# The weight sums of each group's next to last key tile: on GpSimd beside the others, or on VectorE behind the step's maxima

## The chip, the cores and the metric

The kernel runs on one core of one Trainium2 chip. The metric is the device time of one execution, in microseconds. Three executions of the kernel before took 1801.5, 1802.37 and 1805.26 us, so its median is 1802.37 us. One more execution was profiled, and every view below comes from that one.

The engines are named as in the profile: PE is TensorE's matmul row and PEld its weight loads, DVE is VectorE, ACT is ScalarE, POOL is GpSimd.

## The reference, cut to what matters

Two layers work on x, a tensor of 2 x 1024 rows of 512 numbers in float32. The first layer adds a small scan block and a gated feed-forward block with a Walsh-Hadamard transform. The second adds causal attention with 16 heads of 32 and a gated feed-forward block with two-of-four sparsity. The change lies in the attention:

```
scores = einsum('bqhe,bkhe->bhqk', q, k) * scale
scores = where(causal, scores, -inf)
attn = softmax(scores, axis=-1)
out = einsum('bhqk,bkhe->bqhe', attn, v)
out = out.reshape(b, l, d) @ W_out.T + b_out
```

The softmax is not formed before it is used. The kernel multiplies v with the unnormalized weights exp(score - maximum), adds the weights up beside that, and divides at the end. The additions of the weights are what the change moves.

## The kernel before, in words

The program has three stages: the first layer (to 658 us of the span), the attention with its projections (658 to 1215 us), and the sparse feed-forward block (to the end).

The attention works on units. A unit u is one batch and one group of four heads, so there are eight units, 0 to 7. Within a unit the queries come in two halves j of 512 columns, and the keys in tiles kt of 128 rows. By the causal mask half 0 meets key tiles 0 to 3 and half 1 meets key tiles 0 to 7, which makes twelve steps per unit (`per` is 12) and 96 steps in all. Step (u, 1, 6) is the next to last of a unit. A unit lasts some 62 us and a step some 5.2 us.

The main loop `for n in range(-ahead, len(second))` writes out one step after another, and `in_program_order` then pins that order on PE, DVE, ACT and POOL: each of these engines executes its own instructions in the order in which the loop wrote them. One pass of the loop does this:

- `weights(u, j, kt)` computes the scores of the step in two PSUM pairs of two heads each (PE `s`, L1226 and L1232). ACT writes their exponentials into two tiles `pt` (L1243), for kt = 0 into the two tiles `acc`. From the query column s on, tiles on the diagonal need the causal mask: POOL sets the forbidden half of a 128 x 128 block to zero with `affine_select` (L1252, two of them per step). For half 1 these are kt = 4 to 7. Half 0 is masked in all its steps, so the mask of a unit's first step works on the new `acc`.
- `gather(*behind)` takes the weights of the step before: PE multiplies them with v into the bank `o` (L1272), and for kt > 0 the two tiles are added to the sums, acc += pt (L1279). For key tile 6 only columns 256 to 511 of the two heads are added, 128 x 512 elements per tile. When a half is done, ACT copies `o` to `att` (L1282).
- `do_first(n + ahead)` runs `maxima` for a step 13 steps ahead: PE scores `m` (L1169), DVE adds the mask on diagonal blocks (L1176) and reduces to `tops` (L1177).
- `one_part(n)` runs a piece of other work, mostly a projection: `pq` (L1122, added up by DVE in L1092 or by ACT in L1087), `pv` (L1047, L1148) or `po` (L1047, L1313). A few passes, named in `quiet`, have none. In three units, the weights of a projection are first combined by four POOL instructions (`sq` and `wqk`, L1099 to L1101 and L1134).
- `what_is_fixed(n)` runs small pieces bound to a step. One is `larger` (L1187), a DVE maximum of 16 columns. It is followed by the `shift_part` pieces on ACT (L1197) and POOL (L1199), and by the transposes `px` (L1207) and their copy `neg` (L1211).

The score pairs of `s` and `m` take turns in three PSUM buffers, so a pair waits until ACT or DVE has read the pair three turns earlier. Parts use one bank, so each waits until the part before has been read. The tiles `pt` have five buffers.

The engine of L1279 is chosen by one line:

```
            if kt:
                eng = nc.vector if idle_vector(u, j, kt) else nc.gpsimd
```

`idle_vector` is true from the point on where no maxima are left, which covers the sums of unit 7. In units 0 to 6 all the sums that the change can touch are on POOL. There, one step of half 1 gives POOL two masks and two sums in this order: the masks of a step, then the sums of the step before.

Of the kernel before, what the change touches and what calls it, by code (L numbers as in the profile page):

```python
# [35 lines left out]
def two_layers(ctx: ExitStack, tc: tile.TileContext, t: dict, out: bass.AP):  # L36
    nc = tc.nc
# [37 lines left out]
    def ps_bank(name, which):  # L75

        return ps.tile([P, 512], F32, tag=f"bank{which}", name=name)
# [278 lines left out]
    with tc.tile_pool(name="a", bufs=1) as a:  # L356
# [431 lines left out]
        for n in range(NU - 1):  # L788
            u = 2 * n + 2
# [162 lines left out]
    with tc.tile_pool(name="b", bufs=1, reuse_waits="tile") as b:  # L952
# [207 lines left out]
        def maxima(u, qt, c):  # L1160

            q, k = qk[u, 0], qk[u, 1]
            if qt == 0:
                tops[u] = sm.tile([P, 2, QT, 4], F32, tag="tops", name=f"tops_{u}", bufs=2)
            e = min((qt + 1) * P - c * 512, 512)
            pair = [ps_wide(f"m_{u}_{qt}_{c}_{p}") for p in range(2)]
            for h in range(4):
                rows = slice(h * HD, (h + 1) * HD)
                nc.tensor.matmul(  # L1169
                    pair[h // 2][:, h % 2, :e], q[rows, qt * P : (qt + 1) * P],  # L1170
                    k[rows, c * 512 : c * 512 + e], start=True, stop=True,
                )
            for p in range(2):
                if c == qt // 4:
                    d = pair[p][:, :, e - P : e]
                    nc.vector.tensor_add(d, d, mask.unsqueeze(1).to_broadcast([P, 2, P]))  # L1176
                nc.vector.tensor_reduce(  # L1177
                    out=tops[u][:, c, qt, 2 * p : 2 * p + 2], in_=pair[p][:, :, :e],
                    axis=mybir.AxisListType.X, op=ALU.max,
                )  # L1180
# [32 lines left out]
        def idle_vector(u, j, kt):  # L1213

            return per * u + 4 * j + kt + ahead >= len(second)
# [40 lines left out]
                got.append(pt)  # L1256
            return u, j, kt, s, got

        held, sums_of = {}, {}

        def gather(u, j, kt, s, pts):

            bb, hg = units[u]
            if kt == 0:
                held[u, j] = ps_bank(f"o_{u}_{j}", 0)
                sums_of[u, j] = pts
            po = held[u, j]
            last = kt == 4 * j + 3
            v = vals[bb, kt // NJ, kt % NJ][:, hg * P : (hg + 1) * P]
            for h in range(4):  # L1270
                rows = slice(h * HD, (h + 1) * HD)
                nc.tensor.matmul(  # L1272
                    po[rows, s:], v[:, rows], pts[h // 2][:, h % 2, s:],
                    start=(kt == 0), stop=last, tile_position=(0, h * HD),
                )
            if kt:
                eng = nc.vector if idle_vector(u, j, kt) else nc.gpsimd
                for acc, pt in zip(sums_of[u, j], pts):
                    eng.tensor_add(acc[:, :, s:], acc[:, :, s:], pt[:, :, s:])  # L1279
            if last:  # L1280
                att[u, j] = b.tile([P, 512], F32, tag="att", name=f"att_{u}_{j}", bufs=12)
                nc.scalar.copy(att[u, j], po)  # L1282
# [136 lines left out]
        def do_first(n):  # L1419
            u, qt, c = first[n]  # L1420
            maxima(u, qt, c)
# [3 lines left out]
        def one_part(n):  # L1425

            if not open_parts:
                ready = [x for x in rest if x[0] <= n]
                if not ready:
                    return False  # L1430
                x = min(ready, key=lambda x: x[1])
                rest.remove(x)
                open_parts.extend(x[2])
            f, *args = open_parts.pop(0)
            f(*args)
            return True

        def what_is_fixed(n):
            for f, *args in fixed.pop(n, ()):
                f(*args)  # L1440
                if f == total:
                    for q in range(4):
                        put(n + 1, divide, *args, q)

        def late(n):

            return any(
                sum(len(x[2]) for x in rest if x[0] <= n and x[1] <= last) + len(open_parts)
                > last - n
                for last in {x[1] for x in rest}  # L1450
            )
# [9 lines left out]
        for n in range(-ahead, len(second)):  # L1461
            if n == 0:
                alone = None
            now = weights(*second[n]) if n >= 0 else None
            for f, *args in middle.pop(n, ()):
                f(*args)
            if behind is not None:
                gather(*behind)
            behind = now
            for f, *args in after.pop(n, ()):  # L1470
                f(*args)
            if n < 0:
                one_part(n)
            if n + ahead < len(first):
                do_first(n + ahead)
            if (n >= 0 or n % 2) and n not in quiet:
                one_part(n)
            while late(n) and one_part(n):
                pass
            what_is_fixed(n)  # L1480
        in_program_order(start)
        gather(*behind)
        alone = 0
        n = len(second)
# [13 lines left out]
    with tc.tile_pool(name="c", bufs=1, reuse_waits="tile") as c_:  # L1498
# [131 lines left out]
        for n in range(groups - 1):  # L1630

            end = n == groups - 2
            u = 2 * n + 2
# [165 lines left out]
```

## Time and profile before

| | before |
|---|---|
| median of three executions | 1802.37 us (1801.5 to 1805.26) |
| the profiled execution | 1803.46 us, span 1801.7 us |
| PE busy | 1776.1 us (99%) |
| DVE busy | 1141.5 us (63%) |
| ACT busy | 480.2 us (27%) |
| POOL busy | 847.8 us (47%) |
| POOL sums (L1279) | 138, 233.7 us |
| DVE sums (L1279) | 22 |
| mean granted TensorE clock | 0.998 |

The span runs from the first to the last instruction in the trace; the profiled execution's own time is 1.76 us longer, which is what lies around the span. A busy share is of the span. A row of the timeline gives start, duration, engine, line, operation, output <- inputs, shape and count, and in brackets the idle time of the engine before it with what ended it. Line numbers are those of the kernel before. A row may join several instructions of one kind.

### The profile page before, as it was taken

The numbers are of one execution on the slowest core, as the hardware profiler recorded it, in microseconds if no ns is written. First come the engines' busy times: TensorE is split into PE (matmuls) and PEld (weight loads), VectorE is DVE, ScalarE is ACT, GpSimd is POOL, SyncE is SP. The second block draws the span as 40 slices with busy tenths as digits, with TensorE's granted clock in tenths as the row PEclk, the third lists the DMA queues.
The fourth block names the chain that finished last, engine by engine and source line by source line (L and its number), as shares of the span: only waits on it lengthen the run. The fifth ranks groups of instructions, "written<-read, shape, count | busy, mean of one in ns | idle before, by whom it ended". The sixth has DMA issues, their size and how long they took to land.

```text
span 1801.7 us, 19007 instructions
## 1 busy us (share of the span) xinstructions
PE 1776.1 (99%) x7354; PEld 910.9 (51%) x7354; DVE 1141.5 (63%) x1502; ACT 480.2 (27%) x687; POOL 847.8 (47%) x741
## 2 busy tenths in 40 slices
PE   9999999999999999999999999999999999999999
PEld 5456566555555564333333333334555555555555
DVE  4875444555544457566666666762867778778676
ACT  3322222122221113433433433422212211212220
POOL 5145553355642244577868866613243344342510
PEclk9999999999999999999999999999999999999999
DMA  6120110111101010000000000011110102211101
GB/s 234 47 82 24 49 45 25 35 35 35 35 24 35 12 41 13 1 12 13 1 24 25 13 12 1 25 47 35 35 59 28 54 24 70 84 34 47 47 1 47
DMA packets 29609, 68.12 MB, mean 38 GB/s; under 512 B 3408, under 2 KB 11856, under 8 KB 27984
## 3 DMA queue, kind: packets, MB, share of 16 engines
q1 hardware_dynamic: 28800, 66.61, 11.1%
q8 instruction: 59, 0.97, 0.2%
q10 hardware_dynamic: 720, 0.30, 0.1%
q14 instruction: 30, 0.25, 0.0%
HBM read 62.70 MB, written 4.19 MB: 37 GB/s over the span
## 4 chain that ended last, share of the span: by engine, by line
PE 90%; POOL 4%; DVE 3%; ACT 1%; issue 1%; POOLq 0%; ACTq 0%; DVEq 0%
PE p_a L183 22%; PE p_c L183 21%; PE d L309 19%; PE m L1169 4%; PE s L1226 3%; PE pv L1047 3%; PE po L1047 3%; PE o L1272 3%; POOL acc L1279 3%; PE pq_a L1122 2%; PE dr L1620 2%; PE pq_c L1122 1%; DVE tops L1177 1%; PE pp L607 1%; PE pw L443 1%
## 5 line engine op out<-in xcount | busy, mean ns | idle before, releaser
L327 POOL TENSOR_TENSOR x<-x,de 128x512 f32<-128x512 f32 x87 | 126.6, 1469 | 297.8 <-DVE x L322 162.5
L1279 POOL TENSOR_TENSOR acc<-acc,pt 128x1024 f32<-128x1024 f32 (+3 forms) x138 | 233.7, 1717 | 0.0
L1177 DVE TENSOR_REDUCE tops<-m 128x2 f32<-128x1024 f32 (+2 forms) x192 | 180.9, 956 | 52.3 <-PE m L1169 47.7
L322 DVE TENSOR_TENSOR x<-x,d 128x512 f32<-128x512 f32 x145 | 99.2, 685 | 143.2 <-PE d L309 142.9
L1243 ACT ACTIVATE pt<-s 128x1024 f32<-128x1024 f32 (+3 forms) x160 | 115.4, 766 | 191.1 <-PE s L1232 174.3
L309 PE MATMUL d<-td,h 128*128 128x256 f32 x592 | 139.2, 379 | 0.0
L309 PEld LDWEIGHTS d<-td,h 128*128 128x128 f32 x592 | 112.5, 190 | 42.6 <-issue 28.7
L183 PE MATMUL p_a<-xt,s_a 128*128 128x512 f32 x256 | 116.6, 598 | 0.0
L183 PE MATMUL p_a<-xt,w 128*128 128x512 f32 x256 | 115.4, 593 | 0.7 <-ACT xt L136 0.7
L183 PE MATMUL p_c<-xt,gu 128*128 128x512 f32 x256 | 115.7, 592 | 0.0
L183 PE MATMUL p_a<-t_a,s_a 128*128 128x512 f32 x256 | 115.3, 594 | 0.0
L183 PE MATMUL p_c<-xt,s_c 128*128 128x512 f32 x256 | 115.1, 592 | 0.0
L1169 PE MATMUL m<-qk,qk 32*128 32x512 f32 (+3 forms) x768 | 104.8, 542 | 4.1 <-ACT acc L1243 3.0
L1176 DVE TENSOR_TENSOR m<-m,mask 128x256 f32<-128x256 f32 x128 | 54.8, 428 | 84.3 <-PE m L1169 76.1
L1226 PE MATMUL s<-qk,qk 32*128 32x512 f32 (+3 forms) x768 | 98.2, 532 | 3.5 <-DVE tops L1177 2.3
L176 POOL TENSOR_TENSOR s_c<-gu,s_c 128x512 f32<-128x512 f32 x16 | 20.4, 1274 | 132.4 <-PE p_c L183 132.4
L1169 PEld LDWEIGHTS m<-qk,qk 32*128 32x128 f32 x768 | 40.4, 184 | 73.6 <-issue 25.0
L183 PEld LDWEIGHTS p_a<-xt,s_a 128*128 128x128 f32 x256 | 47.2, 190 | 57.8 <-issue 57.4
L183 PEld LDWEIGHTS p_c<-xt,s_c 128*128 128x128 f32 x256 | 48.6, 190 | 51.5 <-issue 50.2
L183 PEld LDWEIGHTS p_c<-xt,gu 128*128 128x128 f32 x256 | 48.6, 190 | 51.0 <-issue 49.5
L183 PEld LDWEIGHTS p_a<-xt,w 128*128 128x128 f32 x256 | 48.4, 190 | 50.1 <-issue 47.6
L1226 PEld LDWEIGHTS s<-qk,qk 32*128 32x128 f32 x768 | 34.0, 183 | 78.5 <-issue 67.5
(286 smaller groups left out, 3236.3 us busy)
## 6 DMA issues: line engine op xcount, KB each, us to landing
w<-in_W SPq DMA_DIRECT2D x32, 512.0 KB, 3.5
gu<-in_gu SPq DMA_DIRECT2D x32, 512.0 KB, 3.5
wd<-in_down SPq DMA_DIRECT2D x8, 1024.0 KB, 4.8
x<-in_x SPq DMA_DIRECT2D x16, 256.0 KB, 4.2
w2h<-in_W2q SPq DMA_DIRECT2D x4, 1024.0 KB, 12.0
xr<-in_x SPq DMA_DIRECT2D x16, 256.0 KB, 2.6
wqk<-in_WqkvT SPq DMA_DIRECT2D x16, 256.0 KB, 3.1
out_x<-x SPq DMA_DIRECT2D x15, 256.0 KB, 2.0
```

Source lines behind the costliest of these rows:

```text
L183: nc.tensor.matmul(pair[:, m, :], a[:, m, k, :], x[:, k, :], start=start and k == 0, stop=stop and k == 1, skip_group_check=True,)
L309: nc.tensor.matmul(out_[:, j, :], lhs[:, q, j * P : (j + 1) * P], rhs[:, q], start=m in (0, 1, 3, 4) and j == q == 0, stop=j == q == 1, sk ...
L322: nc.vector.tensor_add(r, r, out_)
L327: nc.gpsimd.tensor_add(r, r, u2[half])
L1047: nc.tensor.matmul(got[0], lhs(k), rhs(k), start=(k == 0), stop=(k == KC - 1))
L1122: nc.tensor.matmul(got[chain], lhs[:, k, :], rhs[k] if type(rhs) is list else rhs[:, k, :], start=start and k == 0, stop=stop and k == 1, ...
L1169: nc.tensor.matmul(pair[h // 2][:, h % 2, :e], q[rows, qt * P : (qt + 1) * P], k[rows, c * 512 : c * 512 + e], start=True, stop=True,)
L1176: nc.vector.tensor_add(d, d, mask.unsqueeze(1).to_broadcast([P, 2, P]))
L1177: nc.vector.tensor_reduce(out=tops[u][:, c, qt, 2 * p : 2 * p + 2], in_=pair[p][:, :, :e], axis=mybir.AxisListType.X, op=ALU.max,)
L1226: nc.tensor.matmul(pair[h // 2][:, h % 2, s:], k[rows, kt * P : (kt + 1) * P], q[rows, cols], start=True, stop=False,)
L1243: nc.scalar.activation(pt[:, :, s:], pair[p][:, :, s:], AF.Exp, scale=1.0 / math.sqrt(HD))
L1279: eng.tensor_add(acc[:, :, s:], acc[:, :, s:], pt[:, :, s:])
```

## The change

The sums of key tile 6 in half 1 of units 0 to 6 are no longer written out by `gather` on POOL. They are kept in a list, and the main loop writes them out on DVE after the maxima of the same pass, ahead of that pass's part. All other sums stay where they were, and so do the masks. In the written order, `larger` comes behind the sums in units 0 to 5, since it is written out at the end of the pass; in unit 6 it is written out one step earlier and stays ahead of them.

```diff
-        held, sums_of = {}, {}
+        held, sums_of, add_later = {}, {}, []
+
+        def add_weights(eng, u, j, s, pts):
+            for acc, pt in zip(sums_of[u, j], pts):
+                eng.tensor_add(acc[:, :, s:], acc[:, :, s:], pt[:, :, s:])
...
-            if kt:
-                eng = nc.vector if idle_vector(u, j, kt) else nc.gpsimd
-                for acc, pt in zip(sums_of[u, j], pts):
-                    eng.tensor_add(acc[:, :, s:], acc[:, :, s:], pt[:, :, s:])
+            if (j, kt) == (1, 6) and not idle_vector(u, j, kt):
+
+                add_later.append((nc.vector, u, j, s, pts))
+            elif kt:
+                add_weights(nc.vector if idle_vector(u, j, kt) else nc.gpsimd, u, j, s, pts)
...
             if n + ahead < len(first):
                 do_first(n + ahead)
+            while add_later:
+                add_weights(*add_later.pop())
             if (n >= 0 or n % 2) and n not in quiet:
                 one_part(n)
```

## The prediction, made blind

> **What bounds the kernel now.** I read the page's busy times first, then busy time by stage, then the chain that ended last around a unit boundary, and last the timelines of PE, POOL and DVE at the boundaries.
>
> ```profile
> PE 1776.1 (99%) x7354; PEld 910.9 (51%) x7354; DVE 1141.5 (63%) x1502; ACT 480.2 (27%) x687; POOL 847.8 (47%) x741
> ```
> ```profile
> 658.00:1215.00 557.00, 538.86 (x3392) 193.59 (x3391) 370.10 (x530) 204.83 (x323) 361.90 (x358) 0.99 0.05 16
> ```
>
> PE sets the time. In the attention (second fence: length, then PE, PEld, DVE, ACT, POOL) it is idle for 557.00 - 538.86 = 18.1 us, so a change to POOL and DVE can bring only part of that, and whatever makes PE wait costs in full. The chain shows where POOL reaches PE, the boundary of units 0 and 1:
>
> ```profile
> 785.41 2.46 POOL acc L1279 x2
> 790.73 0.37 POOL acc L1252
> 791.14 1.41 PE o L1272 x8
> ```
>
> Half 1 gives POOL more work than a step holds: it falls behind, and the first mask of the next unit comes late. The timelines there (PE, POOL, DVE):
>
> ```profile
> 791.14 1.41 PE L1272 MATMUL o<-acc,v 128*32 128x512 f32 x8 [0.74 <-POOL acc L1252]
> ```
> ```profile
> 784.65 0.77 POOL L1252 TENSOR_SCALAR_AFFINE_SELECT pt<-pt 128x256 f32<-128x256 f32 x2
> 785.38 2.50 POOL L1279 TENSOR_TENSOR acc<-acc,pt 128x512 f32<-128x512 f32 x2
> 787.83 0.73 POOL L1099 TENSOR_TENSOR sq<-wqk 128x256 f32<-128x256 f32 x1
> 790.68 0.76 POOL L1252 TENSOR_SCALAR_AFFINE_SELECT acc<-acc 128x256 f32<-128x256 f32 x2
> ```
> ```profile
> 784.09 0.65 DVE L1187 TENSOR_TENSOR tops<-tops 128x16 f32<-128x16 f32 x1
> 786.69 0.43 DVE L1176 TENSOR_TENSOR m<-m,mask 128x256 f32<-128x256 f32 x1 [1.96 <-PE m L1169]
> ```
>
> PE wants the masked acc at 790.40 and gets its first tile at 791.09. It waits 0.74 us, and the two tiles come 0.36 us apart, so the group takes 1.41 us instead of 1.06 as at 852.56. The same stands at 914.96 and 1039.01 (0.76 idle, 1.41 long): the three boundaries where the weight sums (L1099 to L1134) lie before that mask. At 1/2, 3/4 and 5/6 they do not, and POOL is in time: at 850.89, where PE asks at 852.56.
>
> **Off POOL.** The sums are the 128x512 form: half of its 28 instructions on POOL (1276 ns). Fourteen go, 17.9 us busy, 2.46 us per boundary. Only three boundaries wait for them, each for 0.75 + 0.35 = 1.1 us: 3.3 us on the path. Everything else there hides behind PE.
>
> **Onto DVE.** The same form costs on DVE:
>
> ```profile
> L1279 DVE TENSOR_TENSOR acc<-acc,pt 128x512 f32<-128x512 f32 x4 | 2.6, 685 | 0.0
> ```
>
> Fourteen times 0.685 is 9.6 us. They lie where DVE has finished its maxima (784.16) and idles until 786.69, so by length they fit. But they need POOL twice. The first needs POOL's sum of key tile 5 for its own tile (done 782.9), the second the other one (784.70). And both operands lie in SBUF, which the trace shows to be slow beside POOL: `larger`, 16 columns, took 0.165 us at 725.5 with POOL idle, and here:
>
> ```profile
> 907.82 1.44 DVE L1187 TENSOR_TENSOR tops<-tops 128x16 f32<-128x16 f32 x1
> 908.47 0.76 POOL L1252 TENSOR_SCALAR_AFFINE_SELECT pt<-pt 128x256 f32<-128x256 f32 x2
> ```
>
> It ended at 909.26, when POOL's second mask ended (909.23). At 784.09, 1031.87 and 1093.51 it ended with POOL's running sum instead, ahead of the masks; issued during the first mask (847.25, 971.07) it waited for the second too. So DVE gets in at the end of a POOL sum, mostly, and not between two masks.
>
> The Trainium skill, "SBUF — State Buffer", section "Who interferes with whom", says that a DVE instruction with two SBUF inputs and a GpSimd instruction that reads SBUF exclude each other, the later one blocked until the first ends. It speaks against this change, and these rows agree. By the rule taken whole, the masks wait for a whole sum (0.69 us); the total below would then be 1.3 us higher, 1799.9 us.
>
> Step by step at boundary 0/1: the first DVE sum starts with POOL's release at 784.70 and holds the pair for about 0.5 us. That is my estimate: in unit 7 a 256-column DVE operation stretched POOL's pair of sums from 2.50 to 2.68 us, and 685 ns is the upper end; bounds 0.2 and 0.7. The masks of key tile 7 end at 785.9 instead of 785.41. The second DVE sum follows to 786.5, `larger` behind POOL's next instruction to about 787.3. The next maxima start 0.6 us late. PE asks for their first buffer at 789.8, and they free it at 788.5 instead of 787.85: covered, with 1.2 us left. The part's bank at 1/2 and 3/4 (DVE L1148 now behind the sums) is free at 849.4 where PE asks at 849.62: covered by 0.2 us only.
>
> The late masks reach PE: key tile 7's `o` starts at 785.59, its second half at 785.72. Masks 0.5 later hold the second half by 0.24 us, of which 0.18 is hidden, since the next `m` waits until 786.76 for ACT anyway. That leaves 0.06 us, seven times: 0.4 us. Its bounds are nothing (masks first) and 7 x 0.6 = 4.2 us (both sums ahead of the second mask).
>
> What is late next: POOL's queue to the acc mask is now two sums' holds (1.0 to 1.25) and 787.83 to 791.44 (3.6), from 785.4, so it ends by 790.25, the first tile by 789.9. PE asks at 790.40 and 790.7. The stall goes whole, with half a microsecond to spare.
>
> **Unit 7.** Here POOL's sums fight DVE's masks:
>
> ```profile
> 1155.27 2.68 POOL L1279 TENSOR_TENSOR acc<-acc,pt 128x512 f32<-128x512 f32 x2
> ```
> ```profile
> 1155.82 2.41 DVE L1248 TENSOR_TENSOR acc<-acc,allowed 128x256 f32<-128x256 f32 x2 [1.65 <-ACT acc L1243]
> ```
> ```profile
> 1157.34 2.00 PE L1272 MATMUL o<-acc,v 128*32 128x512 f32 x8 [0.42 <-ACT att L1282]
> ```
>
> The pair of masks takes 0.75 us at 1158.86 with POOL idle, 2.41 here. After the change DVE's sums run from 1154.4 to 1156.2 (behind POOL's key tile 5), the masks from 1156.8 to 1157.5, and `o` takes 1.06: it ends at 1158.4 instead of 1159.34. I take 0.9 us; bounds 0 (the later waits for ACT at 1171.71 and DVE at 1179.92 eat it) and 0.9.
>
> **The sum.** 1803.46 - 3.3 - 0.9 + 0.4 = 1799.7 us for the profiled execution. The median stands 1.1 us lower: 1802.4 - 3.8 = 1798.6 us, 0.21% faster. About 0.2% (3.6 us) is what a measurement of this kernel can tell from no change, so the forecast lies just beyond that line.
>
> **Rivals.**
>
> *Slower: POOL keeps the pair until its queue is dry.* At the three boundaries with weight sums POOL runs without a pause from 784.7 to 793.9. If DVE waited that long, the sums would end at 795.2, the first maximum at 796.3 where PE asks at 789.8: 6.5 us, three times, 19.5 - 3.8 gives 1818 us. PE pays as soon as a sum ends 1.2 us later than above; 0.2% slower takes 2.5 us more than that at each of three places, 1806 us. For: the wait at 907.82 lost its turn once. Against: no `larger` waited past the second mask. Chance 0.18 for 1806 to 1818.
>
> *No gain: the second sum gets in between the masks.* Key tile 7's `o` is held 0.6 us in seven units, 4.2 instead of 0.4: 1802.4 us. For: in unit 7 DVE and POOL alternate from one instruction to the next. Against: three times of three `larger` did not come between two masks. Chance 0.20, from 1800.5 to 1804.
>
> *Faster: slow clock windows go too.* The windows view, cut at the points where the granted clock changes (last but two numbers: clock):
>
> ```profile
> 854.39:857.80 3.41, 2.32 (x28) 1.01 (x28) 2.69 (x4) 0.92 (x3) 3.41 (x5) 1.00 0.00 0
> 857.80:861.21 3.41, 3.41 (x10) 1.03 (x9) 1.59 (x3) 0.35 (x2) 3.41 (x5) 0.50 0.02 5
> 789.53:792.95 3.42, 2.68 (x28) 0.80 (x24) 0.57 (x1) 1.67 (x3) 3.42 (x7) 1.00 0.00 0
> ```
>
> A stretch with PE busy 2.32 of 3.41 us is followed by one at half the clock, which cost 0.81 us in its `m` (1.96 for 1.15) and 0.84 in its `pv` (2.82 for 1.98): 1.65 us. The same stands at 980.68. The stretch at 789.53 with 2.68 is not followed by one. The cause of the two is a 1.09 us wait of PE for DVE at 856.09 and 979.91, which the change leaves, but moves 1.1 and 2.2 us earlier. If one or both then straddle a cut, 1.65 to 3.3 us go: 1797 to 1795.3 us. Chance 0.15; where the cuts fall may differ in each execution, so I leave it out of the sum. The Trainium skill, "TensorE: Matmul & The Clock Gate", section "What's actually happening", has this window free-running and asks for an idle window before the clock falls; here a window still two thirds busy did it.
>
> **How the numbers follow.** The forecast has 0.47, of which I put 0.38 beyond the line: its bounded terms cut both ways, but with two slow windows already there, the clock will rather lower it. Faster: 0.38 + 0.15 = 0.53. Within 0.2%: 0.09 + 0.20 = 0.29. Slower: 0.18. The range from 1795.0 to 1804.0 takes in all but the slower rival; the forecast's own is 1797 to 1801.
>
> **What would show it.** Right: `o<-acc` at the starts of units 1, 3 and 5 takes 1.06 us with no idle before it; POOL loses 17.9 us busy, DVE gains 9.6 plus its waits; key tile 7's masks end at most 0.5 us later; `o<-acc` of unit 7 takes 1.06. Wrong: DVE sums longer than 2 us, PE idle before key tile 7's `o` or `m`, before `s` by DVE tops in more places than 856 and 980, or before `pv` by DVE v.

## The result, and the profile after

The kernel after took 1799.18 us in the median of twelve executions (1796.52 to 1802.16), the kernel before 1803.10 us in twelve beside it (1801.32 to 1805.58). The ratio is 0.9975, with a 95% interval of 0.9967 to 0.9983: 0.25% or 4.5 us faster. The profiled execution of the kernel after took 1798.73 us, span 1797.0 us, against 1803.46 and 1801.7 before. The prediction was 3.8 us faster.

The page of the kernel after, busy times:

```profile
PE 1772.6 (99%) x7354; PEld 909.9 (51%) x7354; DVE 1153.1 (64%) x1516; ACT 480.3 (27%) x687; POOL 836.0 (47%) x727
```

POOL lost fourteen instructions, but only 11.8 us of busy time instead of 17.9, and DVE gained 11.6 instead of 9.6. The missing time is where the two engines hold each other up: POOL's masks (L1252) together take 4.3 us longer than before, and the boundary of units 0 and 1 shows how. In the timelines of the kernel after, `o` is L1276, the sums are L1263. POOL, then DVE:

```profile
784.52 1.69 POOL L1252 TENSOR_SCALAR_AFFINE_SELECT pt<-pt 128x256 f32<-128x256 f32 x2
786.18 0.72 POOL L1099 TENSOR_TENSOR sq<-wqk 128x256 f32<-128x256 f32 x1
789.04 0.77 POOL L1252 TENSOR_SCALAR_AFFINE_SELECT acc<-acc 128x256 f32<-128x256 f32 x2
```
```profile
783.96 1.98 DVE L1263 TENSOR_TENSOR acc<-acc,pt 128x512 f32<-128x512 f32 x2
787.36 0.43 DVE L1176 TENSOR_TENSOR m<-m,mask 128x256 f32<-128x256 f32 x1 [1.12 <-PE m L1169]
```

The two masks of key tile 7 take 1.69 us where they took 0.77: DVE's first sum went in at the end of POOL's sum, ahead of the first mask, and its second one between the masks. So the masks end at 786.2, not at 785.4. DVE is done at 786.24, `larger` included, and still idles 1.12 us before the next maxima. The acc mask, the one that PE waited for, starts at 789.04 instead of 790.68. PE there, before and after:

```profile
785.95 1.52 PE L1169 MATMUL m<-qk,qk 32*128 32x256 f32 x8
```
```profile
786.27 0.41 PE L1276 MATMUL o<-pt,v 128*32 128x128 f32 x4 [0.39 <-POOL pt L1252]
786.61 0.73 PE L1169 MATMUL m<-qk,qk 32*128 32x256 f32 x8
787.27 1.98 PE L1122 MATMUL pq_a<-xt,wqk 128*128 128x512 f32 x4
790.20 1.07 PE L1276 MATMUL o<-acc,v 128*32 128x512 f32 x8
```

PE now waits 0.39 us for the late mask, and yet `pq_a` starts at 787.27, as early as before (787.39, with the kernel after already 0.12 us ahead at this point). The next row explains it. Before, `m` took 1.52 us, since its second pair of heads had to wait for ACT and started at 786.76; each pair took 0.70 us. Now both pairs are free when PE gets to them, and they run side by side in 0.73 us. The late mask is paid out of that wait. Then `o<-acc` runs with no idle time, in 1.07 us.

At the boundary of units 1 and 2 (DVE, POOL) the order is another one. Both masks go first, undisturbed, and DVE's first sum waits for them:

```profile
845.06 2.57 DVE L1263 TENSOR_TENSOR acc<-acc,pt 128x512 f32<-128x512 f32 x2
```
```profile
845.71 0.78 POOL L1252 TENSOR_SCALAR_AFFINE_SELECT pt<-pt 128x256 f32<-128x256 f32 x2
```

In this execution units 0, 2 and 4 end the first way, units 1, 3 and 5 the second way. At the start of unit 7, DVE, then PE before and after:

```profile
1147.82 3.09 DVE L1263 TENSOR_TENSOR acc<-acc,pt 128x512 f32<-128x512 f32 x2
1151.43 0.88 DVE L1248 TENSOR_TENSOR acc<-acc,allowed 128x256 f32<-128x256 f32 x2
```
```profile
1154.81 0.77 PE L1272 MATMUL o<-pt,v 128*32 128x128 f32 x8
```
```profile
1150.42 0.41 PE L1276 MATMUL o<-pt,v 128*32 128x128 f32 x4 [0.53 <-POOL pt L1252]
1151.23 0.41 PE L1276 MATMUL o<-pt,v 128*32 128x128 f32 x4 [0.40 <-POOL pt L1252]
1152.59 1.06 PE L1276 MATMUL o<-acc,v 128*32 128x512 f32 x8
```

DVE's pair of masks takes 0.88 us instead of 2.41, and `o<-acc` 1.06 instead of 2.00. But here PE also waits 0.53 and 0.40 us for the late masks of unit 6's key tile 7, and no `m` stands behind that `o`. In return the scores behind it take 1.1 us instead of 1.4, and `o<-acc` no longer waits (0.42 us before). From the scores ahead of all this to the scores behind it PE takes 5.06 us (1148.53 to 1153.59) instead of 5.89 (1153.38 to 1159.27): 0.83 us less.

Setting the starts of the same matmuls side by side gives the ledger. The last column is the step from the line above.

| PE work | start before | start after | after - before | step |
|---|---|---|---|---|
| s, end of unit 0 | 784.30 | 784.18 | -0.12 | |
| pq_a, past the first mask of unit 1 | 793.34 | 792.09 | -1.25 | -1.1 |
| s, unit 2, just behind its wait for DVE | 856.09 | 854.83 | -1.26 | 0 |
| pq_b, unit 2 | 866.24 | 863.88 | -2.36 | -1.1, a slow clock window gone |
| pq_a, past the first mask of unit 3 | 917.69 | 914.19 | -3.50 | -1.1 |
| w, unit 4 | 988.41 | 984.71 | -3.70 | -0.2 |
| pq_a, past the first mask of unit 5 | 1041.21 | 1036.36 | -4.85 | -1.15 |
| s, unit 7 | 1164.01 | 1158.27 | -5.74 | -0.9 |
| po, after unit 7 | 1195.27 | 1190.56 | -4.71 | +1.0, a slow clock window more |
| last stage | 1790.14 | 1785.44 | -4.71 | 0 |

Three boundaries and unit 7 make 4.3 us. One slow clock window less and one more nearly cancel; the rest, 0.1 us ahead of the first row and 0.2 us in units 3 and 4, was not followed up.

### The profile page after: what moved, and what is told of

Its sections match the earlier page's. It is cut to its first block, busy times and chain, and to the rows that moved or that the text cites. A ratio compares the mean times of both kernels' runs of the same rounds, so it can differ in the third digit from the quotient of the medians.

```text
span 1797.0 us, 19003 instructions
## 1 busy us (share of the span) xinstructions
PE 1772.6 (99%) x7354; PEld 909.9 (51%) x7354; DVE 1153.1 (64%) x1516; ACT 480.3 (27%) x687; POOL 836.0 (47%) x727
## 4 chain that ended last, share of the span: by engine, by line
PE 90%; POOL 4%; DVE 3%; issue 2%; ACT 1%; ACTq 0%; POOLq 0%; DVEq 0%
PE p_a L183 22%; PE p_c L183 21%; PE d L309 19%; PE m L1169 4%; PE s L1226 3%; PE pv L1047 3%; POOL acc L1263 3%; PE pq_a L1122 3%; PE po L1047 3%; PE o L1276 3%; PE dr L1627 2%; PE pq_c L1122 1%; DVE tops L1177 1%; POOL pt L1252 1%; PE pp L607 1%
## 5 line engine op out<-in xcount | busy, mean ns | idle before, releaser
L1263 POOL TENSOR_TENSOR acc<-acc,pt 128x1024 f32<-128x1024 f32 (+3 forms) x124 | 216.4, 1770 | 0.0
L1276 PE MATMUL o<-pt,v 128*32 128x512 f32 (+3 forms) x640 | 71.1, 482 | 4.2 <-POOL pt L1252 2.1
```

The lines of the kernel that those rows point to most:

```text
L1276: nc.tensor.matmul(po[rows, s:], v[:, rows], pts[h // 2][:, h % 2, s:], start=(kt == 0), stop=last, tile_position=(0, h * HD),)
```

## The experiments

Each of the ten runs below is told with its ratio to the kernel before, taken beside it, and the 95% interval. Since a single execution can differ by several us from the next (more on that at the last runs), the table also sets executions with the same mean granted clock side by side; the number of executions is in brackets. One slow window of 3.41 us at half the clock is 0.001 of the mean clock of such an execution, so equal clock means about equally many of them.

| kernel | ratio (95%) | at clock 0.999 | at clock 0.998 |
|---|---|---|---|
| before | | 1802.60 (23) | 1804.15 (18) |
| after | 0.9975 (0.9967 to 0.9983) | 1797.96 (2) | 1799.18 (2) |
| units 0, 2, 4 | 0.9974 (0.9963 to 0.9985) | 1799.18 (4) | |
| units 1, 3, 5 | 1.0002 (0.9992 to 1.0012) | 1802.21 (5) | 1803.62 (2) |
| unit 6 | 0.9993 (0.9984 to 1.0002) | | 1802.78 (10) |
| sums left out | 0.9971 (0.9959 to 0.9982) | 1798.01 (4) | |
| ahead of the maxima | 1.0142 (1.0125 to 1.0159) | | |
| before again | 1.0000 (0.9992 to 1.0009) | 1802.56 (5) | 1803.25 (2) |
| weight sums later | 0.9979 (0.9970 to 0.9989) | 1799.52 (3) | 1801.10 (4) |
| att scaled later | 0.9978 (0.9967 to 0.9989) | 1797.09 (1) | 1799.43 (2) |
| no part in pass 5 | 0.9977 (0.9967 to 0.9986) | | 1797.79 (5) |
| no part in pass 1 | 0.9963 (0.9950 to 0.9977) | 1797.19 (3) | 1798.43 (1) |

The theory: PE gains only where it waited for the first mask of a unit behind the weight sums, and at unit 7's masks; all else is hidden. The rivals: any relief of POOL pays; the sums on DVE cost something; the gain comes from fewer slow clock windows.

**One group of units at a time.** The condition in `gather` of the kernel after is changed:

```diff
-            if (j, kt) == (1, 6) and not idle_vector(u, j, kt):
+            if (j, kt) == (1, 6) and u in (0, 2, 4):
```

> The sums of key tile 6 go to DVE in units 0, 2 and 4 alone, ahead of the three boundaries with weight sums. My theory (only PE's wait for the first mask of units 1, 3 and 5 pays, and it goes whole): 3 x 1.17 = 3.5 us faster than before, no idle before o<-acc at those starts, and unit 7's o<-acc still 2.0 us long. Rival (any relief of POOL pays in proportion): 3/7 of the change's gain, about 1.9 us.

Measured: 0.9974, and 3.4 us at clock 0.999. Its other three executions, at clock 1.0, are 2.6 us faster than eight of the kernel before at that clock. In its profile the three boundaries are free and unit 7 is not:

```profile
1034.03 1.06 PE L1276 MATMUL o<-acc,v 128*32 128x512 f32 x8
1152.06 2.00 PE L1276 MATMUL o<-acc,v 128*32 128x512 f32 x8 [0.42 <-ACT att L1287]
```

With `u in (1, 3, 5)`:

> The sums of key tile 6 go to DVE in units 1, 3 and 5 alone. My theory: no change (within 0.5 us), since POOL's mask is in time at those boundaries; the waits at the starts of units 1, 3 and 5 stay at 0.75 us. Rival (relief of POOL pays in proportion): about 1.9 us faster. Second rival (the sums on DVE cost PE something): slower by up to 1 us.

Measured: 1.0002 with an interval of 0.1% to both sides, 0.4 to 0.5 us faster at equal clock. The wait stays:

```profile
1039.62 1.41 PE L1276 MATMUL o<-acc,v 128*32 128x512 f32 x8 [0.79 <-POOL acc L1252]
```

With `u == 6`:

> The sums of key tile 6 go to DVE in unit 6 alone. My theory: 0.8 us faster than before, all of it at o<-acc of unit 7 (1.06 instead of 2.0 us), since POOL's last sums no longer alternate with DVE's masks. Rival (the later waits of unit 7 for ACT and DVE eat it): no change.

Measured: 0.9993. The interval reaches past 1, so the ratio alone doesn't tell 0.8 us from nothing; at clock 0.998 it is 1.4 us. The profile tells: the masks' alternation with POOL's sums is gone and `o<-acc` takes 1.06 us.

```profile
1157.94 1.06 PE L1276 MATMUL o<-acc,v 128*32 128x512 f32 x8
```

Relief of POOL in proportion is out: equal numbers of sums in units 0, 2, 4 and in units 1, 3, 5 bring about 3 us and nearly nothing.

**No sums at all.** In the kernel after:

```diff
-                add_later.append((nc.vector, u, j, s, pts))
+                pass
```

> The sums of key tile 6 in units 0 to 6 are left out altogether, on POOL and on DVE. My theory (what the sums do on DVE, the late masks of key tile 7 with them, costs PE nothing): the time of the change, 4.3 us faster than before. Rival (the shared access costs PE): faster than the change by the 0.4 us that I had put down for the late masks, or by more.

Measured: 0.9971, at clock 0.999 1798.01 against 1797.96 of the kernel after. What the sums cost on DVE, with the late masks, the waits for POOL and 11.6 us of busy time, is nothing that these runs can tell.

**Ahead of the maxima.** In the kernel after:

```diff
-                add_later.append((nc.vector, u, j, s, pts))
+                add_weights(nc.vector, u, j, s, pts)
```

> The sums of key tile 6 go to DVE in all seven units, but ahead of the maxima of the same pass. My theory (the place behind the maxima is what hides DVE's wait for POOL): DVE waits at 782.3 for POOL's sum of key tile 5 until 784.6 and for the masks after that, so the maxima start about 4 us late and PE waits for them with its next scores, 2.7 us in each of the six units that have maxima there: 16 us less 4.3, some 12 us slower than before. Rival (DVE has room anyway): 4.3 us faster, like the change.

Measured: 1.0142, 27 us slower between the medians, where I had put 12. DVE, then PE, at the boundary of units 0 and 1:

```profile
786.16 3.09 DVE L1263 TENSOR_TENSOR acc<-acc,pt 128x512 f32<-128x512 f32 x2 [0.64 <-POOL acc L1263]
789.17 0.42 DVE L1176 TENSOR_TENSOR m<-m,mask 128x256 f32<-128x256 f32 x1
```
```profile
790.20 0.70 PE L1226 MATMUL s<-qk,qk 32*128 32x512 f32 x2 [1.58 <-DVE tops L1177]
793.61 3.78 PE L1122 MATMUL pq_a<-xt,wqk 128*128 128x512 f32 x4
```

The same two sums, waiting the same way, now stand in front of the maxima. PE waits 1.58 us and some more within the group: from its start to the next `o` it takes 4.11 us (787.49 to 791.60) where it took 1.29 before (784.30 to 785.59), 2.8 us more where I had put 2.7. What I had not put in is the second row: `pq_a` takes 3.78 instead of 1.98 us, at half the clock. In this profile a stretch at half the clock begins within 3.2 us of the end of each of the six waits, and the mean clock fell to 0.988. Six times 2.8 us less 4.3 is 12.5 us; the other 15 or so are what the lower clock would cost by the line worked out at the next run. So the direction and the wait were right, and the price was less than half, for want of the clock.

**The kernel before again.**

> The kernel before, unchanged, to read its times together with the granted clock of each execution. My theory (slow clock windows, which come and go by chance, spread the times of one kernel): no change against before; 1.2 to 1.7 us of time for each 0.001 of mean clock; at equal clock 3.8 to 4.7 us slower than the change. Rival (the change is faster because it has fewer slow windows): at equal clock before and after would stand within 1 us of each other.

Measured: 1.0000. The executions of the kernel before that were taken beside the runs (65) give 1.48 us for each 0.001 of mean clock; the twelve of the kernel after give 1.35. At the same clock before and after differ by 4.7 us at 0.997 (13 and 3 executions), 5.0 at 0.998, 4.6 at 0.999 and 4.2 at 1.0 (8 and 3), where I had expected 3.8 to 4.7. The mean clock is 0.9983 before and 0.9981 after. So the gain is not one of clock, and the clock is what spreads the executions of one kernel.

**All sums on POOL, the weight sums later.** In the kernel before, `part` of `project`, for the units behind the first:

```diff
-                    weight_sums(w11, w21, w22)
+                    if u == 0:
+                        weight_sums(w11, w21, w22)
...
-                if n == 0:
+                if u and n == 1:
+                    weight_sums(w11, w21, w22)
+                if n == (1 if u else 0):
                     nc.gpsimd.tensor_sub(w12, w12, got[2])
```

> The kernel before with all sums on POOL; instead, the four weight sums of a projection (L1099 to L1134) are written out with its second piece rather than with its first, so that the next unit's first mask stands ahead of them on POOL. My theory (the weight sums in front of that mask make PE wait): 3.5 us faster than before, with POOL's busy time unchanged and no sum moved to DVE. Rival (POOL's total load is what counts): no change.

Measured: 0.9979, at equal clock 3.1 us. All three boundaries are free:

```profile
1035.02 1.07 PE L1275 MATMUL o<-acc,v 128*32 128x512 f32 x8
```

POOL is busy 848.8 us, as much as before (847.8). The order on POOL alone is enough for most of the gain; unit 7 keeps its 2.00 us. The 0.4 us that are missing from 3.5 were not followed up.

**Another late mask.** In the kernel after, for half 0 of units 0 to 6, the product att x inv is put one pass later:

```diff
-            if q == 3:
-                nc.gpsimd.tensor_mul(att[u, j], att[u, j], inv[u, j])
+            if q == 3 and not (j == 0 and u < len(units) - 1):
+                scale(u, j)
+
+        def scale(u, j):
+            nc.gpsimd.tensor_mul(att[u, j], att[u, j], inv[u, j])
...
+                    if j == 0 and u < len(units) - 1:
+                        put(n + 3, scale, u, j)
```

> The kernel after, and besides the product att x inv of half 0 (POOL, 1.27 us, ahead of the masks of key tile 6) is written out one pass later, behind the sums of key tile 5. In before and after, o of key tile 6 takes 0.98 us where the same form takes 0.64 elsewhere, because its masks come late. My theory: that wait is on the path, 0.34 us in seven units, so 2.4 us faster than the change and 6.7 faster than before. Rival (it is hidden behind the next scores, as the late masks of key tile 7 are): the time of the change.

Measured: 0.9978, at equal clock within 0.9 us of the kernel after. My theory fell; the rival held, for another reason than it gave:

```profile
782.38 0.64 PE L1276 MATMUL o<-pt,v 128*32 128x256 f32 x8
783.50 0.50 PE L1169 MATMUL m<-qk,qk 32*128 32x128 f32 x8 [0.48 <-DVE tops L1177]
```

`o` of key tile 6 does take 0.64 us, and PE then waits 0.48 us for DVE's maxima of the pass before. Two waits ended at nearly the same point; taking one away uncovered the other.

**Away from the wait that slows the clock.** The kernel after, with `quiet`, the list of passes without a part, changed:

```diff
-        quiet = {per * u + n for u, n in ((0, 6), (2, 1), (2, 6), (4, 1), (4, 6), (5, 6))}
+        quiet = {per * u + n for u, n in ((0, 6), (2, 4), (2, 6), (4, 4), (4, 6), (5, 6))}
```

> The kernel after, with one more edit: the passes without a part in units 2 and 4 are the fifth (key tile 0 of half 1) instead of the second (key tile 1 of half 0). In the second pass PE waits 1.09 us for DVE's maxima of 768 elements, and that wait is what sets off slow clock windows in units 2 and 4; in the fifth the maxima are over 128 columns. My theory: up to 1.09 us less in two units and fewer slow windows there: 1 to 2 us faster than the change at equal clock, up to 2.7 more on top where a slow window no longer comes. Rival (the wait moves to the new place, for ACT's exponentials of the first tile): the time of the change, with a wait of about 1 us in the fifth pass.

Measured: 0.9977. At clock 0.998 it is 1.4 us faster than the kernel after (five and two executions); the 1.09 us wait is gone, and one of 0.42 us has come:

```profile
868.95 1.49 PE L1226 MATMUL s<-qk,qk 32*128 32x512 f32 x8 [0.42 <-ACT acc L1243]
```

But its mean clock was lower (0.9967 against 0.9981), so the forecast of 1 to 2 us at equal clock held, the one of fewer slow windows did not, and by its ratio the kernel is no faster than the kernel after. With (2, 0) and (4, 0) instead:

> As the run before, but the passes without a part in units 2 and 4 are the first (key tile 0 of half 0), whose maxima are over 256 columns. My theory: the wait shrinks as well, but the first mask of the new acc is then wanted 2 us earlier and POOL has it late: between 0.5 us faster and 1 us slower than the change. Rival (the maxima alone set the wait): about 1 us faster than the change, as with the fifth pass.

Measured: 0.9963, the lowest ratio of all, 0.8 us faster than the kernel after at equal clock. That is past the 0.5 us that I had allowed, and closer to the rival: in the first pass of unit 4 PE waits 0.21 us for ACT (976.21), and `o<-acc` (978.08) follows with no wait for a late mask. Its interval overlaps that of the kernel after, and only five executions stand behind it: it beats the kernel before, and probably but not surely the kernel after.

## Why the prediction was right

The sum was 3.3 + 0.9 - 0.4 = 3.8 us; the ledger has 3.4 + 0.9 with nothing more taken off, 4.3. By its terms:

- **The three boundaries** (3.3): right, in place and size. The steps are 1.1, 1.1 and 1.15 us, and the runs on single groups of units show that of the six boundaries these three alone pay. The spare time at the acc mask was there as forecast: the second tile was done at 789.81 where PE began at 790.20, though each mask of key tile 7 and each DVE sum had stretched the other.
- **Unit 7** (0.9): right in size, 0.9 in the ledger, and `o<-acc` takes 1.06 us as written. The way to it was not foreseen whole: I had left out the 0.93 us that PE waits for the late masks there, and the waits behind them that go. They make up for each other, since PE would have waited anyway: with the sums left out altogether the stretch of 5.06 us takes 4.95 (1148.72 to 1153.67), with 0.42 us of waiting ahead of `o<-acc`. That these two cancel was luck. DVE's masks ran from 1151.43 to 1152.31; the forecast, moved by the 4.9 us gained up to there, had them from 1151.9 to 1152.6.
- **The late masks** (0.4 against): this term was mis-sized. The order that I had called a rival came true in units 0, 2 and 4, with both sums ahead of the second mask, and I had priced it at 0.6 us a place. There it cost nothing, though the masks ended 0.8 us later than before (786.21 instead of 785.42) where I had allowed 0.5, and PE's wait ahead of key tile 7's `o` was one of my signs of being wrong. In unit 6 the late masks cost 0.1 us, by the comparison just made. I had let the second pair of `m` follow the first one, when the two pairs, held up together, run side by side: 0.73 us for both instead of 1.52.
- **The DVE side:** the first sum took 1.97 us in units 1, 3 and 5, close to the 2 us that I named as the limit, and 2.28 us at 1147.82, beyond it; the cover held: DVE still idles 1.12 us at the first boundary. The part's bank at 1/2 was the tightest, and PE did not wait for it. The run with the sums ahead of the maxima shows what this cover is worth.
- **POOL's and DVE's busy time:** forecast as -17.9 and +9.6 plus waits, measured as -11.8 and +11.6. An instruction that waits for the shared access counts as busy, on both engines.
- **The slower rival** did not come: in this profile no DVE sum waited past the second mask. It was nearer than that sounds. In the profile with units 0, 2 and 4 alone DVE's two sums at the end of unit 2 waited for the masks and for two weight sums as well:

```profile
905.48 3.81 DVE L1263 TENSOR_TENSOR acc<-acc,pt 128x512 f32<-128x512 f32 x2
```

They end at 909.29, and PE's scores at 910.77 are 0.34 us longer than in the kernel after (1.36 to the next `o`, instead of 1.02). So DVE can wait into POOL's queue, but these runs show no case near the 6.5 us of the rival.

- **The faster rival**, the slow clock windows: one of the two went, but another came elsewhere. Below are the windows of the kernel after, cut where its clock changes (the cuts lie 3.41 us apart).

```profile
851.12:854.54 3.42, 2.62 (x28) 0.80 (x20) 1.25 (x2) 1.67 (x3) 3.42 (x5) 1.00 0.00 0
854.54:857.95 3.41, 3.12 (x25) 1.22 (x26) 1.86 (x4) 1.25 (x3) 3.21 (x4) 1.00 0.02 5
974.00:977.42 3.42, 2.33 (x24) 1.12 (x28) 2.52 (x4) 0.93 (x3) 0.95 (x3) 1.00 0.00 0
977.42:980.83 3.41, 3.41 (x17) 0.95 (x10) 0.49 (x2) 1.05 (x3) 2.87 (x4) 0.50 0.01 2
```

The first 1.09 us wait now lies across the cut at 854.54, PE is busy 2.62 and 3.12 us on its two sides, and no slow window follows. The second lies within one window, 2.33 us busy, and one follows. A further one came at 1175.39 in unit 7. The mean clocks of before and after are alike, so it was right to leave this out of the sum.

## What to carry to other kernels

A long queue on a helper engine costs only where its last entry is what the bound engine asks for; find that place, and either shorten the queue ahead of it or put the wanted entry first. Here putting four POOL instructions later, at three places, brought some 3 of the 4.5 us that moving fourteen to DVE brought. Work put on a second engine belongs behind what the bound engine asks of that engine next: the same sums cost nothing behind the maxima and 27 us ahead of them. And before pricing a wait, look whether a later instruction already waits for something else: three times here one wait was hidden in another, twice in favour of the kernel and once against the experiment.

## What the runs showed of the hardware that I had not expected

- Slow clock windows explain most of the spread between executions. A stretch of 3.41 us with PE busy 2.32 or 2.33 us was followed by one at half the clock; stretches with 2.62 and 2.68 were not. By mean clock, the kernel after took 1796.67 us at 1.0 and 1802.01 at 0.996.
- When a DVE sum waits beside POOL's pair of masks, it goes ahead of both in units 0, 2 and 4 (then alternating with them) and behind both in units 1, 3 and 5, though it starts 0.6 to 0.7 us before POOL's sum ends in each. The unit does not decide it: with units 0, 2 and 4 alone DVE waits behind both masks in units 2 and 4, and in the run with no part in pass 5 it goes ahead in units 1 and 3 and waits in units 0, 2 and 4. What decides it stays open.
